# A shorter first batch in an attention kernel: cheaper slot formula, sums shared with VectorE, output weight loaded later

## The chip, the cores and the metric

The kernel runs on one core of one Trainium2 chip. The metric is device time in microseconds (us), lower is better. The core has five engines with a queue of instructions each, which run side by side and wait for one another by semaphores: TensorE (PE, with its weight loads as PEld), VectorE (DVE), ScalarE (ACT), GpSimd (POOL) and SyncE (SP, whose queue issues most DMA transfers).

## The reference

Sixteen batches of 1024 tokens with 512 channels go through one self-attention layer with 8 heads of 64 channels; keys, queries and values are all the same projection. A mask of zeros and ones says which tokens are active.

```python
xt = jnp.transpose(x, (0, 2, 1))
q = xt @ Wq.T
qh = q.reshape(B, T, NH, dk).transpose(0, 2, 1, 3)
scores = scale * jnp.einsum('bhqd,bhkd->bhqk', qh, qh)
logits = (scores * cmask + (1.0 - cmask) * NEG) * rmask
attn = jax.nn.softmax(logits, axis=-1)
ctx = jnp.einsum('bhqk,bhkd->bhqd', attn, qh)
out = ctx.transpose(0, 2, 1, 3).reshape(B, T, D) @ Wo.T
return x + jnp.transpose(out, (0, 2, 1))
```

A masked key gets weight 0 and a masked query attends evenly to all tokens, so attention need only be computed among the active tokens, about half of them; the masked rows of one batch all get the same added vector, the projection of the mean token.

## The kernel before, in words

Each of the 16 batches is packed: the active tokens are gathered into 512 to 544 slots, attention is done on these, and results are scattered back. The batches are processed in an order found by rank of their active counts.

*Slots.* `slots` (L240) gives each token its place in the packed order: TensorE counts the active tokens ahead of it (`pr`, L250 to L252) and in all (`n`, L255, L256), and VectorE makes the slot from these in small steps (L258 to L268), moves slots from 544 up by 96 (`far`, L267), splits the slot into a block of 128 (`hi`) and a rest (`lo`), and makes one-hot tables; `hot` (L324) compares 128x1024 numbers; `index` (L333, L336) multiplies the tables on TensorE and gets the row numbers. `gather` (POOL, L422) then fetches rows by these, `xt` (L519) transposes them, `xsplit` (L477, L478) makes two 16-bit halves `xh` and `xl`, and `query` (L548, L552) projects them in three products. `facts` (L293 to L317) makes some checks of the counts.

*Opening.* Before the first batch TensorE runs `warm` matmuls (L372) without use of their result. Both weights are loaded (`load`, L180), the query weight in eight halves, the output weight in four blocks, and `split` (L187 on ACT, L190 on DVE) makes 16-bit halves of them. `load_half` (L453) brings x of batch 0 in natural layout in eight pieces, the second four after the first transposes; `sum_half` (L459) sums each on ACT, for the mean token.

*A batch* is 18 steps of a list S, four head pairs p with four query blocks, so that two calls of `scores` make one pair. `scores` (L774) multiplies `xx`, the query halves that four transfers per pair have spread over the partitions (L582 to L585), into banks of PSUM, and four exponentials on ACT follow (L789). `attend` (L809) multiplies them with the values (`value`, L608 or L611, copy L615, squares L594, L598, L599), `attend_tail` copies the context (L832), `recip_sums` and `recip_rows` (L847 to L875) give the divisor through a transpose (L863, copy L868), and `norm` (L911 to L923) applies it. `peaks`, `top` and `bottom` find a shift per head ahead of the exponentials: a transpose (L671) into a spot of PSUM bank 5, a maximum on DVE (`m`, L674), a small matmul (L681), the shift `nm` (L684 to L687), and `corr` on ACT (L695). While batch b runs, the plan calls the next batch's transposes, queries and values between its steps.

*Order.* From the first batch on TensorE's order is written out by hand: `plan` says at which half step what is called, `free` what else is called at a step. The other engines follow the order of a scheduler, steered by `behind` (issue after this instruction) and `high_priority`. `left` holds the four exponentials of the last scores. `needs` adds a wait and `other_banks` says that two instructions that touch the same PSUM tile touch different banks; without it the one waits for the other. PSUM tiles `pm` have two buffers, the tiles `xm` for x in natural layout two as well. In batch 0 `load_all` (L467) brings x of batches 1 and 2, 512 KB a piece, and `sum_half` sums each piece on ACT.

Of the kernel before, what the change touches and what calls it, by code (L numbers as in the profile page):

```python
# [19 lines left out]
P = 128  # L20
# [27 lines left out]
class Fast:  # L48
# [47 lines left out]
    def setup(self, mask_t):  # L96
        nc, const = self.nc, self.const
        B = self.B
        fixed = self.fixed = lambda name, shape, dt=F32: const.tile(shape, dt, name=name)
        self.mt = fixed("mt", [P, B, TB])  # L100
        nc.sync.dma_start(out=self.mt, in_=mask_t)

        self.tri = fixed("tri", [P, P], F16)
        nc.vector.memset(self.tri, 1.0)
        nc.gpsimd.affine_select(out=self.tri, in_=self.tri, pattern=[[1, P]], compare_op=ALU.is_gt, fill=0.0,
                                base=0, channel_multiplier=-1)
        self.on16 = fixed("on16", [P, P], F16)
# [9 lines left out]
        self.kk = iota("kk", [P, NB - 1], [[P, NB - 1]], P, 0)  # L117
        self.ionb = iota("ionb", [P, NB], [[1, NB]], 0, 0)
# [24 lines left out]
        self.place = iota("place", [P, B], [[1, B]], -1, 0)  # L143
        nc.gpsimd.memset(self.place[:, 0:1], float(B - 1))
# [95 lines left out]
    def slots(self, b0, b1):  # L240
# [37 lines left out]
        for b in range(B):  # L278
            nc.vector.tensor_tensor(self.oht[:, b0 + b], oh[:, b * TB:(b + 1) * TB, :],
                                    self.tok.unsqueeze(2).broadcast_to([P, TB, NB]), ALU.mult)  # L280

    def facts(self, b0, b1):
        self.facts_sums(b0, b1)
# [172 lines left out]
    def sum_half(self, b, k):  # L456
        s = self.st[b]
        with self.behind(*self.exp):
            self.nc.scalar.activation(s["xm"][k], s["xm"][k], AF.Copy, accum_out=s["ms2"][:, k:k + 1])  # L459

    def load_all(self, b, c, after=None):

# [204 lines left out]
    def top(self, b, g):  # L667

        nc, s = self.nc, self.st[b]
        pt = self.spot(P)  # L670
        self.spotted(nc.tensor.transpose(pt, self.smcol[g], self.ident))  # L671
        m = s["m"] = self.sb([P, 1], F32, "m", 2)
        with self.tc.high_priority(offset=HPO):
            self.spot_reads += [nc.vector.tensor_reduce(m, pt, AX.X, ALU.max).ins] * self.spots  # L674

    def bottom(self, b, g):

# [64 lines left out]
    def scores(self, b, p, u):  # L742
# [25 lines left out]
                    lanes[k].append((c0, c1, h[:, rows], h[:, cols]))  # L768
        for j in range(max(map(len, lanes))):
            calls += [l[j] for l in lanes if j < len(l)]  # L770
        banks = [c[0] // 512 for c in calls]
        for n, (c0, c1, w, x) in enumerate(calls):
            with self.behind(*last), self.tc.high_priority(offset=HPO if n else 0):
# [9 lines left out]
        self.beat = last[0]  # L783
        self.left, self.context_out = [], None
        ps = {}
        for j in (3, 0, 1, 2):
            k, i, at = places[j]
            t = self.sb([P, C], F32, "p", 12)[:, :A]
            e = nc.scalar.activation(t, flat[:, at:at + A], AF.Exp, bias=s["nm"][p // 2][:, p % 2 * 2 + k:p % 2 * 2 + k + 1],  # L789
# [255 lines left out]
    def run(self, flag):  # L1045
# [42 lines left out]
            self.load("q", c, 0)  # L1088
        for c in range(DC):
            self.load("q", c, 1)  # L1090
        for c in range(DC):
            self.load("o", c)
        halves = [self.split("q", c, h) for h in range(2) for c in range(DC)]
        wide = [self.split("o", c) for c in range(DC)]
        with self.tc.high_priority(offset=HPO):
            self.order()
            self.permute(0, 1)
            self.active(0, 1)
            self.sources(0, 2)
            self.slots(0, 1)  # L1100
        self.warm(9)
        self.hot(0)
        self.index(0)
        for j in range(4):
            self.gather(0, j)
# [1 line left out]
        with self.behind(self.st[0]["at"], self.pe):  # L1107
            with self.tc.high_priority(offset=HPO):
                self.permute(1, 2)
                self.active(1, 2)  # L1110
                self.slots(1, 2)
            for f in halves:
                f()
            with self.tc.high_priority(offset=HPO):
# [5 lines left out]
        for k in range(3):  # L1120
            with self.behind(self.pe):
                self.xt(0, k)
            self.warm(2)
            if k == 0:
                for i in range(DC, 2 * DC):
                    self.load_half(0, i, self.pe)
        def index1():
# [43 lines left out]
        if True:  # L1171
            stack = ExitStack()
            for b in range(B + 1):
# [23 lines left out]
                if n < B:  # L1197
# [21 lines left out]
                    else:  # L1219
# [1 line left out]
                        post = [(0.3, L(self.slots, *g)) for g in new[0]]  # L1221
                        rng0 = [(0, apart(self.range_x, 0, c)) for c in range(DC)]
                        plan = {(0, 0): g1[4:] + query(0, 3, 0) + value(0, 2) + rng0,
                                (3, 0): query(0, 3, 1) + x[:1] + value(0, 3) + pk(b, 1), (4, 0): x[1:2],
                                (5, 0): x[2:3], (5, 1): x[3:],
                                (7, 0): tp(b, 1) + q(0, 0) + bt(b, 1) + q(0, 1), (8, 1): pre + q(1, 0),
                                (9, 1): post, (11, 0): hot + q(1, 1),
                                (12, 0): tc(0) + v(0) + rng[:2] + q(2, 0), (13, 1): index,
                                (14, 0): tv(0) + q(2, 1) + rng[2:] + take[:3], (14, 1): v(1) + q(3, 0) + pk(n, 0),
                                (16, 0): q(3, 1) + tp(n, 0) + take[3:], (16, 1): bt(n, 0),  # L1230
                                (17, 0): v(2) + tc(1) + [(0, L(self.means, n))]}
                else:
# [9 lines left out]
                            (16, 1): P_(3)}  # L1242
                if b in (1, 2):
                    plan[12, 1] += [(0, L(range_w, " oq"[b], c)) for c in range(DC)]
                if b == 1:
                    for c in range(DC):
                        free.setdefault(c, []).append(L(wide_rest, c))
# [3 lines left out]
                for k, x in enumerate([x for x in (b + 2, self.extra.get(b + 2)) if x is not None and x < B]):  # L1251
# [4 lines left out]
                    for c in range(DC):  # L1256
                        at = 3 * c + k + (0 if b else 4)
                        free.setdefault(at, []).append(L(self.load_all, x, c, None if b else first_top))
                        free.setdefault(at + (2 if b + 2 in self.extra else 4), []).append(L(self.sum_half, x, c))
                def fill(st, half):  # L1260
                    for _, f in plan.get((st, half), []):
                        f()
# [175 lines left out]
```

## Time and profile before

| What | Value |
|---|---|
| Median of 3 runs | 974.04 us (973.05 to 974.54) |
| Profiled execution: time, span | 971.93 us, 970.2 us |
| Mean granted TensorE clock | 0.999 |
| Busy: PE, DVE, ACT, POOL | 932.3, 717.7, 650.3, 305.5 us |
| Chain that ended last: PE, DVE, DMA, ACT | 80%, 7%, 5%, 3% |
| PE busy from 48 to 60 us, and from 200 to 400 us | 9.04 of 12 us, 197.19 of 200 us |

Times in the trace count from the start of the span. The span is the profiled part of one execution, 1.73 us less than that execution's own time; the runs without a profile are a little longer. Lines of the trace give the start, the length of one instruction or a merged run of them, engine, line of the kernel, operation, tiles, shapes and, in brackets, how long the engine had been idle and what ended that.

### The profile page before, as it was taken

The numbers are of one execution on the slowest core, as the hardware profiler recorded it, in microseconds if no ns is written. First come the engines' busy times: TensorE is split into PE (matmuls) and PEld (weight loads), VectorE is DVE, ScalarE is ACT, GpSimd is POOL, SyncE is SP. The second block draws the span as 40 slices with busy tenths as digits, with TensorE's granted clock in tenths as the row PEclk, the third lists the DMA queues.
The fourth block names the chain that finished last, engine by engine and source line by source line (L and its number), as shares of the span: only waits on it lengthen the run. The fifth ranks groups of instructions, "written<-read, shape, count | busy, mean of one in ns | idle before, by whom it ended". The sixth has DMA issues, their size and how long they took to land.

```text
span 970.2 us, 22817 instructions
## 1 busy us (share of the span) xinstructions
PE 932.3 (96%) x8124; PEld 580.9 (60%) x8124; DVE 717.7 (74%) x2439; ACT 650.3 (67%) x1677; POOL 305.5 (31%) x309
## 2 busy tenths in 40 slices
PE   7788999999999999999999999999999999999997
PEld 4555666666666666666666566666666656565543
DVE  7768778777677767887688777877877778785664
ACT  5678857666777675776767678665767766565651
POOL 3101023043250522415144150422515135243452
PEclk9999999999999999999999999999999999999999
DMA  7656556466665676756657777654757757555552
GB/s 220 176 154 194 147 168 178 140 189 203 177 197 145 195 199 216 204 147 201 181 177 212 205 234 216 179 164 135 205 159 243 226 153 212 143 163 162 170 179 102
DMA packets 78568, 176.30 MB, mean 182 GB/s; under 512 B 14480, under 2 KB 22416, under 8 KB 78448
## 3 DMA queue, kind: packets, MB, share of 16 engines
q1 hardware_dynamic: 57392, 107.09, 39.2%
q0 software_dynamic: 21056, 67.68, 22.4%
q8 instruction: 66, 1.08, 0.5%
q14 instruction: 54, 0.44, 0.2%
HBM read 91.36 MB, written 33.91 MB: 129 GB/s over the span
## 4 chain that ended last, share of the span: by engine, by line
PE 80%; DVE 7%; DMA 5%; issue 3%; ACT 3%; SPq 1%; POOL 1%; POOLq 0%; DVEq 0%; ACTq 0%
PE pss L809 21%; PE pss L774 17%; PE pm L933 16%; PE pm L548 15%; PE pss L827 2%; PE pm L519 2%; DMA xm<-x_nat_in 2%; DMA xa<-x_in,idx 2%; PE pss L720 1%; PE pm L611 1%; ACT p L789 1%; DVE xl L478 1%; PE pss L933 1%; DVE xa L939 1%; DMA xx<-hl 1%
## 5 line engine op out<-in xcount | busy, mean ns | idle before, releaser
L789 ACT ACTIVATE p<-pss,nm 128x528 f32<-128x528 f32 (+2 forms) x512 | 354.5, 703 | 103.6 <-PE pss L774 101.5
L809 PE MATMUL pss<-p,v 128*64 128x264 f32 (+2 forms) x2048 | 242.4, 389 | 0.0
L774 PE MATMUL pss<-xx 128*128 128x118 f16 (+17 forms) x1856 | 213.0, 287 | 6.0 <-ACT p L789 3.8
L1002 POOL DMA_INDIRECT y_out<-xa,idx x68 | 81.8, 1203 | 409.5 <-DVE nq L686 98.3
L809 PEld LDWEIGHTS pss<-p,v 128*64 128x64 f32 x2048 | 141.4, 137 | 85.9 <-issue 4.8
L774 PEld LDWEIGHTS <-xx 128*128 128x128 f16 (+1 forms) x1856 | 103.2, 96 | 86.4 <-issue 34.3
L548 PE MATMUL pm<-xh,wqh 128*128 128x264 f16 (+5 forms) x512 | 141.8, 277 | 3.2 <-DVE xl L478 1.3
L548 PE MATMUL pm<-xh,wql 128*128 128x264 f16 (+5 forms) x512 | 141.1, 275 | 0.0
L548 PE MATMUL pm<-xl,wqh 128*128 128x264 f16 (+5 forms) x512 | 140.9, 275 | 0.0
L548 PEld LDWEIGHTS <-wqh 128*128 128x128 f16 x1024 | 96.4, 97 | 31.0 <-issue 11.9
L422 POOL DMA_INDIRECT xa<-x_in,idx x68 | 73.5, 1080 | 126.2 <-DMA y_out<-xa,idx 46.4
L789 ACT ACTIVATION_READ_ACCUMULATOR p<-pss,nm 128x1 f32 x512 | 105.4, 206 | 0.0
L933 PE MATMUL pm<-woh,ch 128*128 128x512 f16 x240 | 91.1, 380 | 0.0
L933 PE MATMUL pm<-woh,cl 128*128 128x512 f16 x240 | 90.9, 379 | 0.0
L933 PE MATMUL pm<-wol,ch 128*128 128x512 f16 x240 | 90.9, 379 | 0.0
L552 ACT ACTIVATE q<-pm 128x264 f32<-128x264 f32 (+5 forms) x128 | 51.0, 398 | 45.1 <-PE pm L548 44.9
L615 ACT COPY v<-pm 128x512 f32<-128x512 f32 x64 | 37.5, 587 | 57.9 <-PE pm L611 56.2
L939 DVE SCALAR_TENSOR_TENSOR xa<-pm,xa 128x512 f32<-128x512 f32 x61 | 41.7, 683 | 45.8 <-PE pm L933 45.3
L1002 POOL DMA_INDIRECT y_out<-xi,idx x60 | 64.1, 1068 | 34.3 <-PE pss L720 14.5
L933 PEld LDWEIGHTS <-ch 128*128 128x128 f16 x480 | 44.8, 98 | 47.5 <-issue 4.1
L422 POOL DMA_INDIRECT xi<-x_in,idx x60 | 59.9, 999 | 22.1 <-issue 15.8
L459 ACT ACTIVATE xm<-xm 128x1024 f32<-128x1024 f32 x60 | 64.1, 1071 | 2.0 <-DMA xm<-x_nat_in 1.9
(228 smaller groups left out, 1464.0 us busy)
## 6 DMA issues: line engine op xcount, KB each, us to landing
xm<-x_nat_in SPq DMA_DIRECT2D x60, 512.0 KB
xx<-hl SPq DMA_DIRECT2D x208, 136.0 KB
rb<-rd SPq DMA_DIRECT2D x72, 132.0 KB
xx<-hl SPq DMA_DIRECT2D x48, 128.0 KB
pt<-c SPq DMA_DIRECT2D x36, 132.0 KB
pt<-p SPq DMA_DIRECT2D x36, 132.0 KB
rb<-rd SPq DMA_DIRECT2D x32, 136.0 KB
ub<-ud SPq DMA_DIRECT2D x16, 256.0 KB
```

The source lines that it names most:

```text
L422: dma = self.nc.gpsimd.indirect_dma_start(out=tile[:n], out_offset=None, in_=self.x, in_offset=bass.IndirectOffsetOnAxis(ap=idx, axis=0))
L459: self.nc.scalar.activation(s["xm"][k], s["xm"][k], AF.Copy, accum_out=s["ms2"][:, k:k + 1])
L519: self.pe = nc.tensor.transpose(pt[:, c, :], x[:n, c * P:(c + 1) * P], self.ident[:n, :n]).ins
L548: self.beat = nc.tensor.matmul(pq, lhsT=w[:, c, e * P:(e + 1) * P], rhs=xx[:, c, cols], start=(k == 0), stop=(k == 3 * DC - 1)).ins
L552: nc.scalar.activation(s["q"][:, e, cols], pq, AF.Copy, scale=1.0 / (SX * SW))
L615: nc.scalar.copy(v, pv)
L774: m = nc.tensor.matmul(flat[:, c0:c1], lhsT=w, rhs=x, start=banks[n] not in banks[:n], stop=banks[n] not in banks[n + 1:])
L789: e = nc.scalar.activation(t, flat[:, at:at + A], AF.Exp, bias=s["nm"][p // 2][:, p % 2 * 2 + k:p % 2 * 2 + k + 1], scale=SCALE, accum_out ...
L809: mm = nc.tensor.matmul(pav[k * DK:(k + 1) * DK, g], lhsT=s["v"][p][:, i, k * DK:(k + 1) * DK], rhs=ps[k, i][:, cols], start=(i == 3), sto ...
L933: mm = nc.tensor.matmul(po[:cols.stop - cols.start], lhsT=a[:, e, cols], rhs=w[:, e, :], start=(e == 0 and k == 0), stop=(e == DC - 1 and ...
L939: return self.nc.vector.scalar_tensor_tensor(x, po, 1.0 / (SX * SW), x, ALU.mult, ALU.add).ins
L1002: dma = self.nc.gpsimd.indirect_dma_start(out=self.out, out_offset=bass.IndirectOffsetOnAxis(ap=idx, axis=0), in_=x, in_offset=None)
```

## The change

- A new `slots_of` takes the place of `slots` for batches 0 and 1. With `free` = 1 for a masked token, `sign` = +1 or -1 and `put` = token number if masked, the slot is sign * pr + free * n + put. A second constant `kk_kept` holds the thresholds 128 to 512 and 544 to 928, so that the shift by 96 comes out of the comparison. `n` is counted first. `hot` of batch 0 gets high priority, and six `warm` matmuls run in place of nine.
- The second four pieces of x of batch 0 are loaded after the third transposes, not after the first.
- The output weight is loaded in step 2 of batch 0 and its ACT half split at steps 9, 10, 16 and 17 of it, not at the start.
- In batch 0 the four sums of batch 1's x move from ACT to DVE (`sum_all`).
- The first call of `scores` does one head's two banks first, and its exponentials run in order 0, 1, 2, 3 and not 3, 0, 1, 2.
- `m` in `top` is declared to touch other banks than the exponentials in `left`, in all batches.
- In batch 0's plan the transposes of the next batch's second block move from step 4 to step 5, `index` from (13, 1) to (13, 0), and a query from (14, 0) to (13, 0), ahead of that step's neighbours' scores.

```diff
+        self.kk_kept = fixed("kk_kept", [P, NB - 1])
+        for k, first in ((0, P), (4, C)):
+            nc.gpsimd.iota(self.kk_kept[:, k:k + 4], pattern=[[P, 4]], base=first, channel_multiplier=0,
...
+    def slots_of(self, b):
...
+        nc.vector.tensor_scalar(free, mb, -1.0, 1.0, ALU.mult, ALU.add)
+        nc.vector.tensor_scalar(sign, mb, 2.0, -1.0, ALU.mult, ALU.add)
+        nc.vector.tensor_tensor(put, self.tok, free, ALU.mult)
...
+        nc.vector.tensor_copy(n, pn)
+        nc.vector.scalar_tensor_tensor(base, free, n, put, ALU.mult, ALU.add)
+        nc.vector.tensor_tensor(slot, sign, pr, ALU.mult)
+        nc.vector.tensor_tensor(slot, slot, base, ALU.add)
+        nc.vector.tensor_tensor(ge, slot.unsqueeze(2).broadcast_to([P, TB, NB - 1]),
+                                self.kk_kept.unsqueeze(1).broadcast_to([P, TB, NB - 1]), ALU.is_ge)
+        nc.vector.scalar_tensor_tensor(far, ge[:, :, 4], float(5 * P - C), slot, ALU.mult, ALU.add)
+        nc.vector.tensor_reduce(hi, ge, AX.X, ALU.add)
+        nc.vector.scalar_tensor_tensor(self.lo[:, b], hi, -float(P), far, ALU.mult, ALU.add)
...
+    def sum_all(self, b, c, other):
+        s = self.st[b]
+        if not other:
+            return self.sum_half(b, c)
+        with self.behind(self.last_hl), self.nc.allow_low_precision(reason="float32"):
+            self.nc.vector.tensor_reduce(s["ms2"][:, c:c + 1], s["xm"][c], AX.X, ALU.add)
...
-            self.spot_reads += [nc.vector.tensor_reduce(m, pt, AX.X, ALU.max).ins] * self.spots
+            i = nc.vector.tensor_reduce(m, pt, AX.X, ALU.max).ins
+        if self.spots:
+            self.other_banks(i, *self.left)
+            self.spot_reads.append(i)
...
+        opening = b == 0 and p == 0 and u == 0
+        if opening:
+            calls.sort(key=lambda c: c[0] // (2 * A))
...
-        for j in (3, 0, 1, 2):
+        for j in (0, 1, 2, 3) if opening else (3, 0, 1, 2):
...
-        for c in range(DC):
-            self.load("o", c)
...
-        wide = [self.split("o", c) for c in range(DC)]
+        def wide_high(c):
+            with self.behind(*self.exp):
+                wide.append(self.split("o", c))
...
-            self.slots(0, 1)
-        self.warm(9)
-        self.hot(0)
+            self.slots_of(0)
+            self.hot(0)
+        self.warm(6)
...
-            if k == 0:
+            if k == 2:
                 for i in range(DC, 2 * DC):
                     self.load_half(0, i, self.pe)
...
-                                (3, 0): query(0, 3, 1) + x[:1] + value(0, 3) + pk(b, 1), (4, 0): x[1:2],
-                                (5, 0): x[2:3], (5, 1): x[3:],
+                                (3, 0): query(0, 3, 1) + x[:1] + value(0, 3) + pk(b, 1),
+                                (5, 0): x[1:3], (5, 1): x[3:],
...
-                                (12, 0): tc(0) + v(0) + rng[:2] + q(2, 0), (13, 1): index,
-                                (14, 0): tv(0) + q(2, 1) + rng[2:] + take[:3], (14, 1): v(1) + q(3, 0) + pk(n, 0),
+                                (12, 0): tc(0) + v(0) + rng[:2] + q(2, 0), (13, 0): index + q(2, 1),
+                                (14, 0): tv(0) + rng[2:] + take[:3], (14, 1): v(1) + q(3, 0) + pk(n, 0),
...
+                if b == 0:
+                    for c in range(DC):
+                        free.setdefault(2, []).append(L(self.load, "o", c, None, first_top))
+                        free.setdefault((9, 10, 16, 17)[c], []).append(L(wide_high, c))
...
-                        free.setdefault(at + (2 if b + 2 in self.extra else 4), []).append(L(self.sum_half, x, c))
+                        free.setdefault(at + (2 if b + 2 in self.extra else 4), []).append(L(self.sum_all, x, c, b == 0 and x == 1))
```

More of the change, by code (lines that the diff above doesn't have):

```diff
@@ L117, in setup @@
         self.kk = iota("kk", [P, NB - 1], [[P, NB - 1]], P, 0)
+        self.kk_kept = fixed("kk_kept", [P, NB - 1])
+        for k, first in ((0, P), (4, C)):
+            nc.gpsimd.iota(self.kk_kept[:, k:k + 4], pattern=[[P, 4]], base=first, channel_multiplier=0,
+                           allow_small_or_imprecise_dtypes=True)
         self.ionb = iota("ionb", [P, NB], [[1, NB]], 0, 0)
@@ L280, in slots @@
                                     self.tok.unsqueeze(2).broadcast_to([P, TB, NB]), ALU.mult)
+    def slots_of(self, b):
+        nc = self.nc
+        n = self.n[:, b:b + 1]
+        mb = self.act16[:, b]
+        whole, half = self.sb([P, 7, TB], F32, "c", 4), self.sb([P, TB, 2 * NB], F16, "c", 4)
+        free, sign, put, base, slot, hi, far = (whole[:, k] for k in range(7))
+        ge, oh = half[:, :, :NB - 1], half[:, :, NB:]
+        nc.vector.tensor_scalar(free, mb, -1.0, 1.0, ALU.mult, ALU.add)
+        nc.vector.tensor_scalar(sign, mb, 2.0, -1.0, ALU.mult, ALU.add)
+        nc.vector.tensor_tensor(put, self.tok, free, ALU.mult)
+        pn = self.pm([P, 1])
+        for j in range(TB):
+            nc.tensor.matmul(pn, lhsT=self.on16, rhs=mb[:, j:j + 1], start=(j == 0), stop=(j == TB - 1))
+        pr = self.pm([P, TB])
+        nc.tensor.matmul(pr, lhsT=self.tri, rhs=mb, start=True, stop=False)
+        for s in range(1, TB):
+            self.pe = nc.tensor.matmul(pr[:, s:], lhsT=self.on16, rhs=mb[:, :TB - s], start=False, stop=(s == TB - 1)).ins
+        nc.vector.tensor_copy(n, pn)
[7 more added lines that the diff above has]
+        nc.vector.scalar_tensor_tensor(self.lo[:, b], hi, -float(P), far, ALU.mult, ALU.add)
+        nc.vector.tensor_tensor(oh, hi.unsqueeze(2).broadcast_to([P, TB, NB]),
+                                self.ionb.unsqueeze(1).broadcast_to([P, TB, NB]), ALU.is_equal)
+        nc.vector.tensor_tensor(self.oht[:, b], oh, self.tok.unsqueeze(2).broadcast_to([P, TB, NB]), ALU.mult)
     def facts(self, b0, b1):
@@ L1090, in run @@
             self.load("q", c, 1)
-        for c in range(DC):
-            self.load("o", c)
         halves = [self.split("q", c, h) for h in range(2) for c in range(DC)]
-        wide = [self.split("o", c) for c in range(DC)]
+        wide = []
+        def wide_high(c):
+            with self.behind(*self.exp):
+                wide.append(self.split("o", c))
         with self.tc.high_priority(offset=HPO):
@@ L1110, in run @@
                 self.active(1, 2)
-                self.slots(1, 2)
+                self.slots_of(1)
             for f in halves:
```

## The prediction, made before the changed kernel ran

> **What bounds the kernel now.** I read the page's busy shares, then the busy time by windows, then TensorE's timeline up to 90 us, then the other engines' timelines where TensorE waits.
>
> The windows (length, then busy time of PE, PEld, DVE, ACT, POOL, granted clock, DMA share, GB/s):
>
> ```profile
> 0.00:12.00 12.00, 5.94 (x44) 2.79 (x45) 7.79 (x33) 6.44 (x13) 3.17 (x29) 1.00 0.72 215
> 36.00:48.00 12.00, 8.85 (x66) 5.23 (x65) 8.21 (x23) 8.96 (x25) 0.89 (x1) 1.00 0.66 185
> 48.00:60.00 12.00, 9.04 (x73) 5.86 (x70) 5.81 (x24) 9.43 (x26) 0.00 (x0) 1.00 0.47 128
> 72.00:84.00 12.00, 10.39 (x86) 6.14 (x87) 9.66 (x34) 10.39 (x27) 2.84 (x3) 1.00 0.71 200
> 96.00:200.00 104.00, 101.53 (x909) 64.20 (x907) 80.81 (x272) 72.17 (x185) 19.30 (x19) 1.00 0.57 162
> 200.00:400.00 200.00, 197.19 (x1761) 126.62 (x1760) 146.99 (x483) 137.79 (x355) 69.66 (x66) 1.00 0.63 187
> ```
>
> From 96 us on PE is idle 1 to 3%, so a microsecond won earlier is carried to the end. Before that it idles up to a quarter. Its timeline names the waits (start, length, then in brackets the idle time before it and who ended it):
>
> ```profile
> 21.45 0.66 PE L519 MATMUL pss<-ident,xa 128*128 128x128 f32 x4 [0.73 <-DMA xa<-x_in,idx]
> 33.80 1.14 PE L774 MATMUL pss<-xx 128*128 128x512 f16 x6 [1.40 <-DMA xx<-hl]
> 38.59 1.57 PE L774 MATMUL pss<-xx 128*128 128x512 f16 x8 [1.79 <-ACT p L789]
> 44.04 0.66 PE L519 MATMUL pm<-ident,xa 128*128 128x128 f32 x4 [0.73 <-DVE xl L478]
> 52.29 0.33 PE L863 MATMUL pm<-ident,rcol 128*128 128x128 f32 x1 [1.05 <-DVE xl L478]
> 57.58 0.39 PE L681 MATMUL pss<-ident,m 128*128 128x4 f32 x2 [1.91 <-DVE m L674]
> 73.61 1.58 PE L774 MATMUL pss<-xx 128*128 128x512 f16 x8 [1.75 <-ACT p L789]
> 87.53 0.38 PE L681 MATMUL pss<-ident,m 128*128 128x4 f32 x2 [2.12 <-DVE m L674]
> ```
>
> With the smaller ones PE waits 12.5 us between 21.5 and 88 us; this and the opening are all there is to win. Two of the waits are for L674, which waits itself:
>
> ```profile
> 57.23 0.29 DVE L674 TENSOR_REDUCE m<-pss 128x1 f32<-128x128 f32 x1 [1.91 <-ACT p L789]
> 34.98 0.69 ACT L789 ACTIVATE p<-pss,nm 128x512 f32<-128x512 f32 x1 [1.94 <-PE pss L774]
> 7.07 0.16 DVE L256 COPY n<-pm 128x1 f32<-128x1 f32 x1
> 9.21 1.22 DVE L324 TENSOR_TENSOR tmp<-io,lo 128x1024 f16<-128x1024 f16 x1
> 15.78 1.26 POOL L422 DMA_INDIRECT xa<-x_in,idx x1 [0.30 <-issue]
> ```
>
> The first line is the false tie: m needs L671's transpose, done at 54.3, but waits for exponentials that read other banks. The second: the first exponential waits for all scores. The last three are the opening: small dependent DVE steps, then the gathers.
>
> **Part by part; the lead over the profile of before.**
>
> *Slots.* Before, n to the 128x1024 compare takes 9.21 - 7.07 = 2.14 us. After, the sign product starts when the counts are ready, as n did (7.07); behind it stand two adds at 0.2, a compare at 0.23, far and the sum at 0.28, lo at 0.13: 1.1. Free, sign and put lie beside the counting matmuls. Compare at 8.2: 1.0 us earlier. Nine warm matmuls at 0.427 us (their weight loads' spacing) ended near 10.7, six end at 9.6, so they do not hold the index. Two more iotas of 0.13 us lie in POOL's idle time before 11.65.
>
> *Warm matmuls, weighed.* Weight loads stand 0.43 apart until 11.76 and 0.21 apart from about 12.4, so PE came to full rate near 12 us, after 5 us of nearly unbroken work from 6.9. With six the only gap is 0.1 to 0.3 us at 9.6; I take no cost. [...]
>
> *Opening.* The gathers go out at 10.65 to 14.78, 1 us earlier. The last took 5.63 us to land, against second-half loads of x_nat and 1 MB of output weight; the first at most 4.07. Both rivals for the queues now come later: 14.78 + 4.1 = 18.9. But DVE goes first: eight wql splits in pairs of 0.42 us stand ahead of the first xl. With the index 1.0 earlier, one split moved behind it, setup steps of 0.5 us moved back and index steps of 0.6 us brought forward, I put it at 16.3 (17.69 before), the second at 17.35, the first query matmuls at 18.05, the fourth transposes at 19.45 (21.45). Then the facts (1.1 us of DVE steps behind the third xl) hold L315 until 20.4 against 21.94. Lead: 1.5; bounds 0.7 and 2.1 (facts not in the way).
>
> *First scores.* Banks 0 and 1 need only the first two transfers of xx, so exponentials start near 33.05, when corr is through, instead of 34.98. But on ACT, L552 and the v copy stand ahead of the fourth, and wait for PE's query, which starts only 0.4 us earlier (four matmuls behind the transfer, not six). The fourth ends 0.8 earlier, so do the next scores. Lead 2.3.
>
> *Scores ahead of two transposes (44.5).* They need exponentials only, no longer xl. The scores of 44.54 start when the last exponential ends, 0.8 earlier than 43.75 by the step above: 42.95, without the opening. But the two transposes then stand between them and attend, and ACT's queue (three exponentials, the sum, L832, two xh) shortens by less: at 52.46 it is 0.95 in all instead of 0.8, lead 2.45. The wait of 1.05 stays.
>
> *Tie of L674.* DVE does m when it is transposed; L681 follows the query instead of waiting 1.91. L684 now waits for the exponentials itself, behind it on DVE the steps of recip and the q splits, as they stood behind L674. PE runs two queries meanwhile; their two banks are emptied in time (L552 between and behind the exponentials). Lead 4.35. In later batches m also moves ahead of a few DVE casts; from 100 to 900 us no wait of PE names L674, so I take nothing there.
>
> *Query into the wait of 73.61.* There PE waited 1.75 us for the last of four exponentials. Now twelve query matmuls (1.4 us) run ahead of these scores and no longer behind them, so attend, 76.88 before, comes 1.4 us sooner against the scores; and the exponentials that attend needs lose the 1.07 us sum that stood ahead of them on ACT (74.24), which would else take the bound. With 0.2 from the shorter wait: 1.6. Lead 5.95.
>
> *Sums and output weight.* Four ACT sums (1.07) go, four splits (0.63) come: ACT gains some 1.7 us. Where a split and a sum now both precede L832 (65.9) it is 0.6 later; no scores wait for it. DVE gets four reductions, not in the trace at this shape: above 1.07 (the ACT row), below 1.38 (twice L599's 0.69 for 512); I take 1.3. The first two fall into its idle 3.25 and 3.21 us, the last two (71 and 77) into a stretch with 2 us idle. So DVE holds smcol, L671 and then L681: of the 2.12 at 87.5 only 0.1 is won. On SP the weight loads (1.85 us of issue) move behind the first two xx and around the third, whose readers come 7 us later. SP's xm load now waits for the DVE sum, behind it rd, rb and xx; by these times the sums end before SP reaches it.
>
> Sum: 1.5 + 0.8 + 0.15 + 1.9 + 1.6 + 0.1 = 6.05 us. Span 970.2 - 6.05 = 964.15; the profiled execution, 971.93 with 1.73 around the span, would be 965.9. The runs' median lies 2.1 higher: 974.04 - 6.05 = **968.0**.
>
> **Rivals.**
> 1. *DVE becomes the bound.* For: 43.5 of 48 us busy after the sums in 36 to 84. If the last two sums and L919 behind them delay smcol by what the query and the tie won (3.6), and the opening gives 0.7, some 1.5 us are left: 972.5. Against: the q splits come earlier too.
> 2. *The tie only moves.* L684 waits for the same exponentials; if PE needs its result, or the banks, before the next scores, 3 us less: 971.0. Against: PE's order has only queries there.
> 3. *Half rate lasts.* 13 warm matmuls at 0.427 instead of 2.97 us are 2.6 us more ahead of the first transposes, with a query at half rate up to 3.5: 970.6 to 971.5. [...]
> 4. *Slower.* DVE runs in order, and a sum blocks it until its 512 KB have landed. xm took 4.23 us at 38.73; behind 1 MB of weight at 128 GB/s it can come 8 us later. If the four sums wait 2.5 us each, beyond 1.9 of slack, 8.1 us go on the chain, SP's xx behind them: 976. It decides from 2 us each. Against: the first sum has until 49.3, and I expect its transfer at 45 to 48.5.
> 5. *More:* facts out of the way, and L671 not held: 965 to 966.
>
> **Chances.** Forecast (966 to 970) 0.59; rival 1 0.09, 2 0.14, 3 0.05, 4 0.07, 5 0.06. Range 964 to 972.5: it takes in the opening's bounds, 2, 3, 5 and half of 1. What a measurement tells from no change is 0.2%, 1.95 us: faster 0.59 + 0.14 + 0.05 + 0.06 = 0.84; same 0.09; slower 0.07.
>
> **What would show it.** Right: index near 10.1, L315 near 20.4, first exponential below 32, no wait of L681 near 53, the scores of 73.61 near 69 without a wait above 0.5, batch 1's first scores near 82 (88.0), from there equal idle shares. Wrong: DVE idle ended by xm in 46 to 80, L671 waiting over 2 us for smcol, warm loads 0.43 apart beyond 13, or more PE idle after 96.

## The result, and the profile after

The changed kernel takes 964.4 us (median of 5 runs, 963.45 to 966.12), the kernel before 974.04. The ratio is 0.9905, with a 95% interval of 0.9891 to 0.992: faster, as forecast, and at the low edge of the range of 964.0 to 972.5. The profiled execution took 965.21 us, its span is 963.5 (before 971.93 and 970.2). So two profiles differ by 6.7 us and the medians by 9.6. Both numbers need an explanation, and they have different ones.

The busy time by windows after (same columns as before):

```profile
36.00:48.00 12.00, 9.09 (x69) 5.23 (x68) 7.78 (x23) 9.07 (x26) 0.89 (x1) 1.00 0.83 251
48.00:60.00 12.00, 10.93 (x86) 6.85 (x84) 8.27 (x31) 8.93 (x26) 0.00 (x0) 1.00 0.47 133
72.00:84.00 12.00, 10.96 (x100) 6.75 (x100) 11.89 (x46) 10.15 (x27) 5.01 (x5) 1.00 0.89 270
```

TensorE was busy for 9.04 us of 48 to 60 before; now it is 10.93. In the stretch ahead of it, 36 to 48, little changed (8.85 to 9.09). Its timeline after:

```profile
21.37 0.16 PE L351 MATMUL pm<-eh,on 128*128 128x2 f16 x1 [0.52 <-DVE eh L342]
33.25 1.13 PE L823 MATMUL pss<-xx 128*128 128x512 f16 x4 [1.03 <-DMA xx<-hl]
38.02 1.57 PE L823 MATMUL pss<-xx 128*128 128x512 f16 x8 [1.78 <-ACT p L838]
51.46 0.33 PE L912 MATMUL pm<-ident,rcol 128*128 128x128 f32 x1 [1.07 <-DVE xl L521]
54.68 0.28 PE L727 MATMUL pss<-ident,m 128*128 128x4 f32 x2
70.60 1.58 PE L823 MATMUL pss<-xx 128*128 128x512 f16 x8 [0.32 <-ACT p L838]
81.27 0.33 PE L714 MATMUL pss<-ident,smcol 128*128 128x128 f32 x1 [0.37 <-DVE smcol L708]
82.26 0.38 PE L727 MATMUL pss<-ident,m 128*128 128x4 f32 x2 [0.66 <-DVE m L717]
```

The 1.91 us in front of the first L681 (now L727, at 54.68) are gone, and of the 1.75 us in front of the scores of 73.61 there are 0.32 left (70.60). The 2.12 us in front of the second L681 became 0.37 + 0.66. But the scores of 38.02 still wait 1.78 us for the exponentials, and L351 waits 0.52 us where its predecessor L315 did not wait at all (in e12 below, the kernel before again, it waits 0.39). The lines behind these, from VectorE, ScalarE and GpSimd:

```profile
53.60 0.27 DVE L717 TENSOR_REDUCE m<-pss 128x1 f32<-128x128 f32 x1
56.40 0.16 DVE L730 TENSOR_SCALAR nm<-pss 128x4 f32<-128x4 f32 x1 [1.71 <-PE pm L591]
34.42 0.69 ACT L838 ACTIVATE p<-pss,nm 128x512 f32<-128x512 f32 x1 [2.09 <-PE pss L823]
7.01 0.16 DVE L305 COPY n<-pm 128x1 f32<-128x1 f32 x1
8.58 1.22 DVE L360 TENSOR_TENSOR tmp<-io,lo 128x1024 f16<-128x1024 f16 x1
10.91 1.30 POOL L458 DMA_INDIRECT xa<-x_in,idx  x1 [7.11 <-DVE hr L384]
```

`m` (L717) waits for nothing now. The exponentials' wait is at L730, 1.71 us, and TensorE does not notice it. The first exponential, however, still waits 2.09 us, for the scores: the new order did not let it start early. From n to the 128x1024 compare it takes 8.58 - 7.01 = 1.57 us (2.14 before).

How far the new kernel leads is best read from one `attend` (L809, now L858) to the next, since the start of a run moves by more than 1 us from run to run (n comes between 5.99 and 7.25 us in the profiles below). The starts were 46.62, 62.10, 76.88 and 90.66 us before, and 45.77, 59.10, 72.47 and 85.39 after:

| | n to first attend | first to second | second to third | third to fourth |
|---|---|---|---|---|
| before | 39.55 | 15.48 | 14.78 | 13.78 |
| after | 38.76 | 13.33 | 13.37 | 12.92 |
| gain | 0.79 | 2.15 | 1.41 | 0.86 |
| gain forecast | 2.45 | 1.9 | 1.6 | 0.1 |

With n 0.06 earlier the lead at the fourth attend is 5.27 us (6.05 forecast). It stays between 5.08 and 5.28 until 740 us. Then it grows to 7.4 and ends at 6.7.

### The profile page after: what moved, and what is told of

Read it like the earlier page. It is cut to its first block, busy times and chain, and to the rows that moved or that the text cites. A ratio compares the mean times of both kernels' runs of the same rounds, so it can differ in the third digit from the quotient of the medians.

```text
span 963.5 us, 22790 instructions
## 1 busy us (share of the span) xinstructions
PE 931.5 (97%) x8121; PEld 581.3 (60%) x8121; DVE 721.1 (75%) x2443; ACT 644.7 (67%) x1669; POOL 305.1 (32%) x311
## 4 chain that ended last, share of the span: by engine, by line
PE 81%; DVE 10%; ACT 4%; DMA 2%; issue 2%; SPq 1%; POOL 0%; POOLq 0%; DVEq 0%; ACTq 0%
PE pss L858 22%; PE pss L823 17%; PE pm L982 17%; PE pm L591 16%; ACT p L838 2%; PE pss L876 2%; PE pm L562 2%; DMA xx<-hl 1%; PE pss L766 1%; PE pm L654 1%; DVE xl L521 1%; PE pss L982 1%; DVE xa L988 1%; PE pm L912 1%; DVE p L777 1%
## 5 line engine op out<-in xcount | busy, mean ns | idle before, releaser
L838 ACT ACTIVATE p<-pss,nm 128x528 f32<-128x528 f32 (+2 forms) x512 | 353.9, 702 | 104.7 <-PE pss L823 101.5
L858 PE MATMUL pss<-p,v 128*64 128x264 f32 (+2 forms) x2048 | 242.4, 389 | 0.0
L823 PE MATMUL pss<-xx 128*128 128x118 f16 (+17 forms) x1856 | 213.6, 287 | 3.9 <-ACT p L838 2.8
L858 PEld LDWEIGHTS pss<-p,v 128*64 128x64 f32 x2048 | 141.4, 137 | 85.8 <-issue 4.9
L823 PEld LDWEIGHTS <-xx 128*128 128x128 f16 (+1 forms) x1856 | 103.2, 96 | 85.1 <-issue 34.3
L838 ACT ACTIVATION_READ_ACCUMULATOR p<-pss,nm 128x1 f32 x512 | 105.2, 205 | 0.0
L658 ACT COPY v<-pm 128x512 f32<-128x512 f32 x64 | 37.5, 586 | 56.0 <-PE pm L654 54.3
L881 ACT COPY c<-pss 128x528 f32<-128x528 f32 (+2 forms) x64 | 38.3, 598 | 37.9 <-PE pss L876 26.8
```

Source lines behind the costliest of these rows:

```text
L658: nc.scalar.copy(v, pv)
L823: m = nc.tensor.matmul(flat[:, c0:c1], lhsT=w, rhs=x, start=banks[n] not in banks[:n], stop=banks[n] not in banks[n + 1:])
L858: mm = nc.tensor.matmul(pav[k * DK:(k + 1) * DK, g], lhsT=s["v"][p][:, i, k * DK:(k + 1) * DK], rhs=ps[k, i][:, cols], start=(i == 3), sto ...
L881: self.context_out = nc.scalar.copy(c[:, :A].rearrange("p (g c) -> p g c", g=2), pav).ins
```

## Experiments

They ran on other chips, each beside runs of the kernel before on the same chip: e1 to e8 where that takes 986.6 (e1 to e4) and 986.0 us (e5 to e8), e9 to e11 where it takes 973.7, e12 on a third beside one run of 972.19. Times are ratios to it; the finer reading is the stage lengths of the profiles:

| | n to first attend | first to second | second to third | third to fourth |
|---|---|---|---|---|
| e1, kernel before | 40.16 | 17.16 | 14.77 | 13.78 |
| e2, changed kernel | 39.74 | 13.34 | 13.38 | 12.76 |
| e3, the tie alone | 39.95 | 13.32 | 16.39 | 12.75 |
| e4, all but the tie | 38.68 | 15.51 | 13.37 | 15.50 |
| e5, old plan | 38.28 | 13.32 | 14.77 | 12.75 |
| e6, sums on ScalarE | 38.34 | 13.34 | 13.37 | 12.83 |
| e7, output weight first | 38.46 | 13.33 | 13.37 | 13.02 |
| e8, old slots | 38.85 | 13.34 | 13.38 | 12.76 |
| e9, old first scores | 39.96 | 13.34 | 13.38 | 12.89 |
| e10, first scores freed | 37.96 | 13.33 | 13.37 | 12.84 |
| e11, e10 and VectorE's steps later | 37.92 | 13.34 | 13.37 | 12.85 |
| e12, kernel before | 39.48 | 17.15 | 14.78 | 15.33 |

**e1 and e2: both kernels again.**

> The kernel before, unchanged, profiled and timed once more. Theory A (the gain is TensorE waits removed before 90 us; the rest of the 9.6 us between the medians is chance waits in the second half): batch 1's first scores at 88.0 within 0.2 us, but the waits after 740 us (0.8 for a gather, 0.8 behind L725) come elsewhere or not at all, so the span differs from 970.2 by up to 2 us. Theory B (the late waits belong to the kernel, and the change takes them away): the same waits at 741 to 786 us again, span 970.2 within 0.5.

> The changed kernel, unchanged, profiled and timed once more. Theory A: batch 1's first scores at 82.7 within 0.3 us; the lead from there to 700 us is 5.1 within 0.4; median 6 to 9 us below the kernel before. Theory B: no TensorE wait for a gather or behind L771 after 700 us, and a median 9 to 10 us below.

e1 came to 1.0001 (0.9978 to 1.0025), e2 to 978.47 us and 0.9932 (0.9907 to 0.9958), 6.7 us less than before by the ratio and 8.2 by the medians. Theory B falls in both: the waits at 746 and 778 us are not in e1, and e2 has waits of its own of these kinds (1.13 us behind L771 at 752.58, 1.06 us for a gather at 871.91). But batch 1's first scores missed theory A's numbers too: 90.28 us for 88.0 in e1, 83.56 for 82.7 in e2. What could not be foreseen stands in e1's first-to-second stage, 17.16 us in place of 15.48 with the same wait of 1.91 us, and in e2's first. It is taken up at e12.

**e3 and e4: the tie alone, and everything but the tie.** e3 is the kernel before with this edit, e4 the changed kernel without it:

```diff
-            self.spot_reads += [nc.vector.tensor_reduce(m, pt, AX.X, ALU.max).ins] * self.spots
+            i = nc.vector.tensor_reduce(m, pt, AX.X, ALU.max).ins
+        if self.spots:
+            self.other_banks(i, *self.left)
+            self.spot_reads.append(i)
```

> The kernel before with the declaration on m alone. Theory A: the wait of 1.91 at 57.6 goes, 1.9 to 2.2 us won by the third scores pair (60.6 before); of the 2.12 at 87.5 some 1 us more; 3 us at batch 1's first scores and 3 in the time (971). Theory B: the declaration also wins in each later batch: over 4.5 us in the time, and a lead that grows after 90 us.

> The changed kernel with the false tie of m left in. Theory A: the wait for m is back at 56 us (1.7 to 2) and at 82 us (1 to 2), batch 1's first scores at 85.5 to 86.5, time 3 us over the changed kernel. Theory B: more than 4.5 us over it, growing after 90 us.

e3: 983.02 us, 0.9964 (0.9939 to 0.9989). e4: 983.29 us, 0.9983 (0.9957 to 1.0009). The declaration is worth 15.48 - 13.32 = 2.16 us in the first-to-second stage of the kernel before and 15.51 - 13.33 = 2.18 in that of the changed one, and 13.78 - 12.75 = 1.03 in the third-to-fourth (e3). e4 has both waits back (its L724 is L727 of the changed kernel):

```profile
56.67 0.38 PE L724 MATMUL pss<-ident,m 128*128 128x4 f32 x2 [1.90 <-DVE m L717]
85.38 0.38 PE L724 MATMUL pss<-ident,m 128*128 128x4 f32 x2 [1.67 <-DVE hl L614]
```

In the stages theory A holds for both. The times are too coarse for it: e2 and e4 differ by 4.8 us, 1.6 more than the 3.2 of the two stages, but each of their intervals reaches 2.5 us either way. The growth of theory B is not there, since e4 is 3.8 us behind e2 at the attend of 102 us and 1.3 at that of 348 us. e4's last stage, 15.50 us, is longer than any wait of it explains. The late part of the first two profiles does not come back: here each of the four kernels, with the tie and without, has waits of TensorE of more than 2 us late in the run, near 680 or 856 us, that neither of the first profiles has.

**e5: the old places of transposes, index and query in batch 0's plan.**

```diff
-                                (3, 0): query(0, 3, 1) + x[:1] + value(0, 3) + pk(b, 1),
-                                (5, 0): x[1:3], (5, 1): x[3:],
+                                (3, 0): query(0, 3, 1) + x[:1] + value(0, 3) + pk(b, 1), (4, 0): x[1:2],
+                                (5, 0): x[2:3], (5, 1): x[3:],
...
-                                (12, 0): tc(0) + v(0) + rng[:2] + q(2, 0), (13, 0): index + q(2, 1),
-                                (14, 0): tv(0) + rng[2:] + take[:3], (14, 1): v(1) + q(3, 0) + pk(n, 0),
+                                (12, 0): tc(0) + v(0) + rng[:2] + q(2, 0), (13, 1): index,
+                                (14, 0): tv(0) + q(2, 1) + rng[2:] + take[:3], (14, 1): v(1) + q(3, 0) + pk(n, 0),
```

> The changed kernel with batch 0's old places of the next batch's second transpose, index and query. Theory A (the 1.41 us won between 62 and 77 us are the query matmuls that now fill PE's wait for the last of four exponentials): the wait of L823 near 70 is back at 1.4 to 1.8 us (0.32 in the changed kernel), the third attend starts 1.1 to 1.6 us later than in the changed kernel (72.47) while the second stays within 0.3 of 59.10; time 1 to 2 us more. Theory B (they come from the sum of 1.07 us that left ACT's queue): the third attend stays within 0.4 us of 72.47 and the wait stays below 0.8.

The scores' wait is back, and the second-to-third stage is 14.77, 1.40 us longer, with the stages beside it as in e2. Theory A. The time is 0.9952 (0.9912 to 0.9991).

```profile
70.13 1.57 PE L823 MATMUL pss<-xx 128*128 128x512 f16 x8 [1.74 <-ACT p L838]
```

**e6: the four sums of batch 1's x back on ScalarE.**

```diff
-    ...append(L(self.sum_all, x, c, b == 0 and x == 1))
+    ...append(L(self.sum_half, x, c))
```

> The changed kernel with the four sums of batch 1's x back on ACT. Theory A (ACT's sum ahead of the exponentials near 74 would have taken the bound, so query and sums are won together only): the third attend starts 0.5 to 1.1 us later than 72.47, time 0.5 to 1.5 us more. Theory B (the sums lie beside other work on either engine): first three attends within 0.3 us of 45.77, 59.10 and 72.47; with DVE freed of 2.4 us in 66 to 80 us the second tie's waits (0.37 + 0.66) shrink, and the fourth attend starts 0.3 to 0.8 us before 85.39.

None of the three stages behind the first attend moves by more than 0.09 us: theory A falls, and of B the fourth attend's gain does not come (waits of 0.59 and 0.33 us are left of the 0.37 and 0.66). The time is 0.9925 (0.9896 to 0.9954), the changed kernel's 0.9932. On ScalarE the sum stands for the most part in idle time in front of the exponentials (in the changed kernel ScalarE idled 0.56 us there). These start 0.33 us later behind the scores, but hold nothing: in both kernels the third attend starts 1.87 us behind the scores and takes 3.67 us:

```profile
70.15 1.09 ACT L495 ACTIVATE xm<-xm 128x1024 f32<-128x1024 f32 x1
71.19 0.72 ACT L838 ACTIVATE p<-pss,nm 128x512 f32<-128x512 f32 x1
```

**e7: the output weight loaded and split at the start.**

```diff
+        for c in range(DC):
+            self.load("o", c)
...
+        wide = [self.split("o", c) for c in range(DC)]
```

> The changed kernel with the output weight loaded and split at the start, as before. Theory A (the opening is held by VectorE and not by transfers, so moving 1 MB of loads changed nothing there): the first xl and the first L351 (17.39, 21.37) stay within 0.3 us and all four attends within 0.4 us. Theory B (the loads collide with the gathers): a transpose of the first batch waits over 0.7 us for xa, L351 comes 0.5 to 2 us later, and all attends with it.

From n to the first attend it takes 38.46 us, in the middle of the others with this opening (38.28 to 38.85, e9 and e2 left out), and L351 comes 14.13 us behind n (14.36 in the changed kernel). The first transposes wait 0.50 us for their gather, less than theory B's 0.7. Theory A: moving the load bought nothing; 0.9928 (0.9897 to 0.9958).

**e8: the old slots, nine warm matmuls.**

```diff
-            self.slots_of(0)
-            self.hot(0)
-        self.warm(6)
+            self.slots(0, 1)
+        self.warm(9)
+        self.hot(0)
```

> The changed kernel with the old slot formula, nine warm matmuls and hot without its priority. Theory A (the formula's 0.74 us reach the end of the opening undiminished): index 0.6 to 0.9 us later than 10.39, L351 0.6 to 0.9 us later than 21.37, the first attend 0.5 to 0.9 us later than 45.77 and the rest with it. Theory B (VectorE's queue and the facts hold the opening whatever the index does): index as late, but L351 within 0.3 us of 21.37 and the attends within 0.3 us.

The first gather is 4.58 us behind n (3.90 in the changed kernel), so the formula is worth 0.68 us there. From n to L351 it is 14.38 us, where kernels with the new formula took 13.84 to 14.51 (e9 and e11 left out). So the later gather does not reach L351 clear of the scatter. In every profile but e7's the first transposes start without a gap behind the thirteen `warm` matmuls that stand ahead of them, so their start does not show when the gather landed. That start comes 7.81 to 8.54 us behind n with the new formula (e7 and e9 left out) and 8.63 here. The ratio of 0.9921 (0.9887 to 0.9954) shows no loss.

**e9: the old order of the first scores and exponentials.**

```diff
-        opening = b == 0 and p == 0 and u == 0
+        opening = False
```

> The changed kernel with the old order of the first scores and of their exponentials (3, 0, 1, 2). Theory A (the new order won nothing, since the first exponential waits for all scores of the tile in both): from L351 to the next scores of L823 it takes 16.65 us in the changed kernel (21.37 to 38.02) and 16.5 to 16.8 here. Theory B (the order does win part of the 0.8 us forecast, and something else cost it again): 17.0 us or more here.

966.95 us in a single run, at 973.69 for the kernel before. From L351 to the next scores it takes 16.47 us (16.65 in the changed kernel and in the kernel before): theory A, the new order won nothing. The run also showed rival 3. Its warm matmuls ahead of the first transposes took 4.68 us, not 2.97 (weight loads 0.43 apart up to 16.1 us), the first transposes started 1.74 us later than in the changed kernel and L351 1.38 us later, with everything up to the gathers at the same times:

```profile
12.77 4.68 PE L408 MATMUL warm<-on 128*128 128x512 f16 x13
17.29 0.60 PE L562 MATMUL pss<-ident,xa 128*128 128x128 f32 x4
```

**e10: the first scores freed.**

```diff
+        made = []
...
+            made.append(m.ins)
...
+            if opening:
+                self.other_banks(e, *[m for m, n in zip(made, banks) if n != j])
```

> The changed kernel, with each exponential of the first scores also declared to touch other banks than the matmuls of the other banks, which the forecast had taken for given. Theory A (the forecast's step failed only because that was not declared): the first exponential starts 1.0 to 1.6 us earlier against the first scores (1.17 us behind their start in the changed kernel, 33.25 to 34.42; the idle time of 2.09 us in front of it shrinks to below 1.1), and from L351 to the next scores it takes 15.8 to 16.1 us instead of 16.65; time 0.5 to 0.9 us less. Theory B (the fourth exponential is held by what stands ahead of it on ScalarE, not by the first): the first exponential is earlier, but L351 to the next scores stays at 16.5 or more.

The first exponential starts at 31.07 us, without a wait, 1.52 us ahead of the second half of the scores (32.59) where it was 1.17 behind: 2.7 us earlier against them, more than expected. From L351 to the next scores it takes 16.05 us instead of 16.65 (16.36 to 16.84 in the others, e2 and e11 left out): theory A. The rest of the early start is lost in front of the third and the fourth (here L840 and L824 are the exponentials and the scores, L838 and L823 before the edit):

```profile
33.53 0.69 ACT L840 ACTIVATE p<-pss,nm 128x512 f32<-128x512 f32 x1 [1.03 <-PE pss L824]
35.16 0.38 ACT L595 ACTIVATE q<-pm 128x256 f32<-128x256 f32 x1 [0.85 <-PE pm L591]
36.27 1.58 PE L824 MATMUL pss<-xx 128*128 128x512 f16 x8 [0.71 <-ACT p L840]
```

963.57 us, 0.9895 (0.988 to 0.991). Against the changed kernel's 0.9905 (0.9891 to 0.992) the times don't tell the two apart; the 0.6 us, at least 0.3 against that scatter, are read from the trace.

**e11: e10, with VectorE's steps for later batches and the facts moved behind.**

```diff
-            with self.tc.high_priority(offset=HPO):
-                self.sources(2, B)
...
+        def rows2():
+            with self.behind(self.last_xs):
+                self.sources(2, B)
...
-        first = query(0, 0, 0) + xt(0)[3:] + [(0, L(self.facts, 0, 2))] + query(0, 1, 0) + query(0, 0, 1)
+        first = query(0, 0, 0) + xt(0)[3:] + query(0, 1, 0) + query(0, 0, 1) + [(0, L(self.facts, 0, 2)), (0, rows2)]
```

> The last kernel, and VectorE's steps for the masks of the later batches moved behind the last xs and the facts behind the first three queries. Theory A (these steps held the opening, which is why it gave 0.72 us and not 1.5): from n (L305) to the first xl it takes 9.2 to 9.6 us instead of 9.85 to 10.4, L351 no longer waits 0.52 us, and from n to the first scores it takes 0.8 to 1.5 us less than in the last kernel. Theory B (the transfers of the gathered rows hold the opening): n to the first scores within 0.4 us of the last kernel.

The first xl is 9.80 us behind n (10.17 in e10, 10.38 in the changed kernel, but 9.85 to 9.95 in e2, e5, e6 and e7), and L351, now behind the queries, no longer waits. Yet from n to the first attend it takes 37.92 us, e10's 37.96. Other waits took the place:

```profile
17.58 0.63 PE L562 MATMUL pss<-ident,xa 128*128 128x128 f32 x4 [1.16 <-DVE sc L337]
23.60 0.34 PE L369 MATMUL pm<-oht,tmp 128*128 128x9 f16 x8 [0.41 <-DVE sc L352]
24.84 0.27 PE L591 MATMUL pm<-xh,wqh 128*128 128x258 f16 x1 [0.36 <-DVE idx L372]
```

The third transposes wait 1.16 us. The VectorE step that the line names has no part in these rows; what they can wait for is the landing of their gather, whose issue ended at 13.8 us, but the trace doesn't show it by itself. Later index waits 0.41 us and the query behind it 0.36 for steps of VectorE. Neither theory's numbers came out whole: the first scores start 24.45 us behind n, 0.82 later than in e10 (23.63), where A said earlier and B the same. Only their second half, which waits for its transfer of xx in both, stays (26.49 and 26.53), and the attend with it. 963.62 us, 0.9897 (0.9882 to 0.9912).

**e12: the kernel before, for its clock.**

> The kernel before, unchanged, for one more look at its clock. Theory A (TensorE falls to half rate for single stretches of 3.4 us, mostly right behind its waits of about 2 us, and the kernel before has more of these waits): mean clock 0.995 to 0.997, one to three such stretches in the profile, one of them within 5 us behind the wait of L681 near 57.6 or 87.5; time 972 to 975 us on a chip like the first. Theory B (the stretches have nothing to do with the waits): clock 0.998 or more, or the stretches all beyond 100 us.

973.31 us at a mean clock of 0.996 (972.19 and 0.997 in the run beside it), with two stretches of half rate. The windows (the column before the last two is the granted clock), and the timeline behind the first wait:

```profile
54.00:60.00 6.00, 4.09 (x28) 2.96 (x29) 2.85 (x16) 4.32 (x12) 0.00 (x0) 0.86 0.48 144
60.00:66.00 6.00, 6.00 (x43) 3.52 (x43) 2.95 (x10) 2.98 (x9) 0.00 (x0) 0.85 0.54 157
84.00:90.00 6.00, 3.88 (x32) 2.41 (x31) 5.85 (x20) 3.69 (x11) 2.77 (x3) 0.92 0.84 281
90.00:96.00 6.00, 6.00 (x47) 3.65 (x46) 4.91 (x17) 3.90 (x11) 0.00 (x0) 0.79 0.60 180
```

```profile
57.51 0.39 PE L681 MATMUL pss<-ident,m 128*128 128x4 f32 x2 [1.91 <-DVE m L674]
58.10 0.28 PE L548 MATMUL pm<-xh,wqh 128*128 128x274 f16 x1
58.74 0.43 PE L548 MATMUL pm<-xl,wqh 128*128 128x274 f16 x1
```

Query matmuls of the same shape stand 0.12 us apart at 58.1 and 0.23 apart from 58.5 until 61.7. The clock's record gives both stretches 3.413 us; one begins 0.9 us behind the end of the first wait for L674, the other just at the end of the second (2.12 us, at 89.12). Each costs half its length, 1.7 us, and the stage lengths show it: 17.15 - 15.48 = 1.67 and 15.33 - 13.78 = 1.55. Theory A. The unexplained stages above are the same thing: in e1 and in e4 a stretch behind the wait for the tie, in e3 one behind the scores' wait of 1.74 us, in e2 one from 33.7 us, behind the first scores' waits. Where the profile of the kernel before had none, its waits were as long.

## Why the prediction was right or wrong

The direction and the two largest gains, the tie and the query in the wait, came out with their mechanisms. That 964.4 us lies within the range is luck in part. The low end of the range stood for facts out of the way and L671 not held, of which only a part of the second came; the time got there through the clock and late waits, which the forecast did not have. And of the 2.45 us forecast up to the first attend 0.79 came, which a second tie 0.76 better than forecast half made good.

**From profile to median** (2.9 us of the 3.6 by which the forecast missed). The forecast took the 2.1 us by which the median of before lay above its profile over to the changed kernel, whose median lies 0.8 us *below* its profile. The runs on the later chips point to what this was, the granted clock. The kernel before ran at a mean clock of 0.995 to 0.997 in all nine runs beside e9 to e11, the ten runs of e9 to e11, which lack the waits for the tie, at 0.997 to 0.999. The means, 0.9959 and 0.9985, are 0.0026 x 972 = 2.5 us apart, one and a half stretches. On the chip of e1 to e8 it was 0.9946 over 61 runs of the kernel before, 0.9955 over e1's 12 and 0.9944 over 12 of e4, against 0.9961 in e3 and 0.9967 to 0.9971 in e2 and e5 to e8; there other stretches stand late in the run. So, as an estimate from these means, taking a wait of about 2 us away saves the wait and, in many runs, a stretch of half rate behind it (1.67 us behind the wait of 1.91 in e12). The profile of before was an execution without one (0.999), and that was not seen in it. The changed kernel's five runs in the first measurement were at 0.999 to 1.0. That the other runs of the kernel before had stretches there is concluded from all this, not shown, since their clock is not known.

**After 90 us** nothing was expected, and the change gave nothing: the lead stays between 5.08 and 5.28 us until 740 us. The 1.4 us net that the two profiles gain after that belong to chance: e12, the same code as before, is 3.1 us behind the profile of before up to 740 us and only 1.3 at the end, because two waits of 0.80 and 0.83 us near 746 and 778 us are in that profile and not in e12's.

**Tie of L674:** 2.15 us for 1.9, the mechanism as told; rival 2 falls, since L730's wait of 1.71 us reaches nobody. **Query into the wait:** 1.41 for 1.6, by e5. That the sum on ScalarE would else take the bound was wrong (e6). **Second tie:** 0.86 in the changed kernel and 1.03 in e3 (1.02 in e2), for 0.1. The step that failed is the claim that smcol, L671 and L681 would be held as long as before; VectorE holds them 0.37 + 0.66 us, half of what the forecast itself took, and e6 shows that it is not the sums that hold them. So rival 1 falls; the 43.5 of 48 us that it gave for VectorE does not come out of the rows either, where the 32.33 us busy from 36 to 84 and four sums of 1.3 are 37.5 (38.33 measured). The sums took 1.20 to 1.22 us each (1.3 taken) and only one waited for its transfer, 0.11 us, so that rival 4 falls.

**First scores:** -0.15 us for 0.8, from the first scores (31.57 and 30.85 us) to the next (38.59 and 38.02). The step that failed is "exponentials start near 33.05". They wait for all scores of the tile, as before, because nothing declares their banks apart from the matmuls'; e10 declares it and gets 0.6 of the 0.8.

**Opening:** 0.7 us for 1.5, its lower bound. The slots gave 0.63 at the compare instead of 1.0: the sign product started at 7.23, behind n and another step, and dependent small steps followed at 0.2 to 0.26 us each. The first xl came at 17.39 (16.3 forecast), with the mask steps of the later batches and the weight splits ahead of it on VectorE, and the facts held L351 by 0.52. But the step also lacked limits that were next. The forecast asked whether the `warm` matmuls hold the index, and not whether the thirteen behind it hold the first transposes:

```profile
12.75 2.97 PE L408 MATMUL warm<-on 128*128 128x512 f16 x13
15.55 0.60 PE L562 MATMUL pss<-ident,xa 128*128 128x128 f32 x4
```

The first gather landed 3.50 us after its start, at 14.41 us (15.61 before), but its transposes start at 15.55 (15.78 before): of 1.20 us 0.23 reached TensorE. In e10 and e11 they start 0.92 and 1.00 us behind the landing. This start also goes with the clock: full rate came 2.8 to 3.8 us behind n in e2, e4 and e5, whose first transposes come 7.81 to 7.85 us behind n, but 5.5 us behind n in the changed kernel (8.54) and 9.3 in e9 (10.28). e11 shows that with VectorE's steps out of the way the first xl follows the transposes by 1.36 us (1.83 in e10), and that a transfer and the displaced steps take the time.

What gave the 0.7 us stays open. e7 and e8 lose nothing clear of the scatter without the later weight or the new slots. Left is the later load of the second half of x, which no run takes back alone: with the old load the third or fourth transposes wait 0.63 to 1.06 us for their gather in all four profiles (before, e1, e3, e12), with the new one in two of ten (e4 0.51, e11 1.16).

**Scores ahead of two transposes:** the lead grew by 0.26 from the next scores to L863 (0.15 forecast). **Output weight:** its place is worth nothing, by e7. **Rival 3**, whose longer half rate was the author's assumption, did not come about in the profile after, where the thirteen `warm` matmuls took 2.97 us as before; it did in e9, worth 1.4 us at L351.

## What to carry to other kernels

Read a change by the length of the stages between two fixed points of the work, over several profiles: here two of four repeat within 0.02 us (a stretch of half rate apart) and the last within 0.3, where the total moves by some 5, and an edit in them shows by itself. The opening moves by 0.6 us and more from run to run, and there single edits of that size do not show. A reordering moves nothing as long as a declared or assumed dependency still waits for the whole tile (here 16.65 us from L351 to the next scores with the new order, 16.47 with the old one in e9, 16.05 with the banks declared apart in e10), so look at what the first instruction waits for, not at where it stands. And before a difference between a profile and the median is carried over to another kernel, look at the granted clock in both.

## What the runs showed of the hardware

TensorE fell to half rate (a granted clock of 0.50 from 854 to 856 us in e7) for single stretches of 3.413 us in the middle of dense work, 15 times in the fourteen profiles, most of them right behind a wait of 1.7 to 2.5 us. The profiles that have such stretches, e1 to e4, e7, e8 and e12, ran at mean clocks of 0.993 to 0.997, the other seven at 0.998 or 0.999. In e7 and e8, too, waits of 2.25 to 3.71 us near 673 and 853 us, which the first profiles don't have, go with two such stretches each. Whether a wait does so differs from run to run: 1.91 us had no such effect in the profile of before and had it in e1 and e12.

In e12 the first stretch begins 47.79 us, 14 times 3.413, behind the first release of full rate (10.59 us) and the second 27.31 us, 8 times 3.413, behind the first's end. All 15 begin at such a multiple, and in the first profiles of before and after full rate ended, behind the last matmul, 955.73 and 948.91 us from its release, 280 and 278 times 3.4133. So each profile can be cut into windows of 3.413 us from that release on, 3911 in all without the last 8 us of each. In 12 of them TensorE was busy for at most 1.51 us, so idle for at least 1.9, and behind each of these the clock falls. Of 13 with 1.52 to 1.67 us it falls behind two, of all the others behind one (2.07 us, in e2). In e12 the window from 54.96 to 58.37 holds the whole wait of 55.6 to 57.5, and TensorE is busy for 1.50 us of it. In the profile of before full rate came at 12.08 us, and a bound at 56.45 cuts the same wait into two; the windows beside it have 2.63 and 2.29 us. So the place of the wait in the window tells the cases apart; no run shifted a wait on purpose, so that it is the cause is not shown.
